# One transformer block on one core: unit 0's front made by the generator of the later units, the operand sums of the down weights dealt to other engines, unit 2's statistics and load at other places

## The chip, the core and the metric

The kernel runs on one core of a Trainium2 chip. TensorE (PE) multiplies matrices and transposes; VectorE (DVE), ScalarE (ACT) and GpSimd (POOL) do the element-wise work; the queue of SyncE (SP) issues the transfers. Each engine works through a queue of its own in order, and semaphores hold an instruction until what it needs is done. The metric is the device time of one execution in microseconds (us); lower is better.

## The reference, cut to what matters

All is fp32. `x` is (4, 2048, 512): T = 4 steps of 2048 columns with 512 features. The context has 77 rows of 512 for each of the 4 steps; there are 16 heads of 32.

```python
def _layernorm(x): return (x - mean(x)) / sqrt(var(x) + 1e-5)

def _L0_attn_ref(xs, ...):                    # recurrence over the 4 steps, 64 states
    u = einsum('hk,tbpk->tbph', Vinv * dt, x)
    z = einsum('hk,bpk->bph', V, A * z + u_t) # for each step t
    return 2.0 * ys.real

def _L0_xattn_ref(query, context, Wq, Wk, Wv, Wo):
    scores = einsum('bqhd,bkhd->bhqk', Q, K) / sqrt(32)
    return softmax(scores) @ V @ Wo.T         # heads joined

def _L0_ffn_ref(x, ...):
    h = butterfly(x @ W_exp + b_exp, up_weights)
    h = gelu(h + up_bias)
    h = butterfly(h, down_weights)
    return h @ W_con + b_con + down_bias

x = x + _L0_attn_ref(_layernorm(x), ...)
x = x + _L0_xattn_ref(_layernorm(x), ctx_1024, ...)
x = x + _L0_ffn_ref(_layernorm(x), ...)
```

The butterflies are linear, so they can be multiplied into `W_exp` and `W_con`.

## The kernel before, in words

**Units.** The 2048 columns are cut into 16 units of 128; a unit is one tile `xt` of 128 columns x 4 steps x 512 features. A unit has a *front* (recurrence, cross attention) and a *feed-forward*. The products of a front (queries `q`, output `w`) and the up product are done as seven block products in place of eight; the down product is done with 26 block products out of sums of blocks of either operand.

**Two stretches.** The *opening* (0 to 194.6 us) multiplies the butterflies into the weights (the generator `prep`, made by `_prepare`), makes keys and values, and does unit 0's front and the first part of unit 1's. Then `feed_forward(u)` runs for u = 0 to 15, and between its products it takes one `step()` of the generator `front(u + 1)`, so that PE has the next unit's attention between the products of this one.

**Order.** PE goes in the order of the program throughout. SP and POOL do so in the opening only. DVE and ACT always, and SP and POOL after the opening, are ordered by the framework's scheduler, with some instructions pinned by `keep_in_program_order`.

**Unit 0's front (`front_first`, L646).** It was written by hand, apart from `front`. `normed_pairs` makes the rows for the recurrence one pair ahead (tag `xn`, two buffers), L626 transposes them; `normed` does so for the query rows (L584, L593) and, on ACT, for the final rows (L582). `seven` does the seven query products (L641) with the adds of L676, and POOL changes `b21` (L683) after the second. In attention each of the 4 steps t has four score products (L704); DVE takes the minimum (L707), and ACT does 16 exponentials, each with its sum as a by-product (L709). `divided` takes the reciprocal and multiplies on DVE (L693, L695). Then come transposes of the probabilities (L723), copied to `pt` (L726, L728), and the values (L735). The output products are again `seven`, added to `xt` at L755.

**The other units' front (`front`, L788).** Rows are made two pairs ahead. In attention DVE takes the minimum (L904) and subtracts it (L905), ACT does one exponential over all 16 heads (L908), DVE sums and takes reciprocals (`weighed`, L890), and divides one half of the heads; POOL divides the other (L894). Query product 6 uses a bank of tag "a", the others tag "f". Two sets of transposes are made for one tile `pt`, and values are done two steps at a time. `normed_rows(wait, ...)` makes normalised rows and waits that many steps before it transposes them (L840). `next_stats` takes the next unit's statistics.

**`combine` (L993)** makes the sums of blocks of the normalised rows that the up products read: `t1`, `t2` on DVE, `t3` (L999) and `n4` (L1001) on POOL. For unit 0 it was called after the opening.

**Preparing the weights.** `prep` is stepped through by hand, in turns with `first` (unit 0's front). Its late steps are: the up weights' sums and stores (L474 to L478), 16 groups that multiply the high stages of the down butterfly (L488), 16 sets of transposes (L496, two to a step), and 16 final products (L502, blocks of `wdn`). `evict` copies a bank out; of `share[0]` evictions two are on DVE and the rest on ACT: `share[0]` is 5, and 6 behind the L488 loop.

**The operand sums.** The 26 block products of the down stage need sums of blocks of the down weights: for each j of 0 to 3 two lots of nine (`RIGHT`), made by `_right_sums` (L142 on POOL, L144 on DVE) in two `rings`, and stored by `_right_stores` (L154) to `dn26` in DRAM. Lots use the same two rings again and again, so a lot of j + 1 waits for the store of the same ring for j. j = 0 is made in the opening, and j = 1, 2, 3 in the first three rounds p of unit 0's `feed_forward`. j = 0 and 1 are all on POOL; for j = 2 and 3 the eight sums named in `FAST` are on DVE and ten on POOL.

**Unit 0's up products.** Round p has `up_head` (products 1, 6, 5), `up_mid` (2, 7) and `up_tail` (4, 3), the last one round late (L1028). Product 6 is followed by the add `u2` (L1047), product 7 by `u3` (L1059, L1060). Product 7 of p = 0 is the fifth in the order of PE; it adds into the bank that L1047 reads, and reads `t3`. The weights of rounds 0 and 1 are loaded in the opening (`w_first`, `w_second`), later ones by `up_weights`. Unit 1's query weights (L849) go to the buffer of `w_first`.

Of the kernel before, what the change touches and what calls it, by code (L numbers as in the profile page):

```python
# [17 lines left out]
P = 128  # L18
# [65 lines left out]
FAST = "24", "5", "1", "8", "14", "2", "20", "10"  # L84
# [48 lines left out]
def _right_sums(nc, j, wdn, rings, alone):  # L133

    made = {f"b{k}{d}": wdn[:, 4 * j + k, d * (D // 2) : (d + 1) * (D // 2)] for k in range(4) for d in range(2)}
    for lot, ring in zip(RIGHT, rings):
        w = ring.rearrange("p (s d) -> p s d", s=len(lot))
        for i, (name, x, op, y) in enumerate(lot):
            made[name] = w[:, i, :]
            x, y, op = made[x], made[y], ALU.add if op == "+" else ALU.subtract  # L140
            if alone or name not in FAST:
                nc.gpsimd.tensor_tensor(made[name], x, y, op)  # L142
            else:
                nc.vector.tensor_tensor(made[name], x, y, op)  # L144
# [215 lines left out]
def _prepare(nc, keep, pool, room, late, banks, dram, ident, wexp_t, up_low, up_high, up_bias, dn_low, dn_high, wcon,  # L360
# [122 lines left out]
    nc.sync.dma_start(out=brow[1, :].rearrange("(p m) -> p m", m=NB), in_=b2)  # L483
    for c in range(NC):
# [7 lines left out]
    share[0] = 6  # L492
# [22 lines left out]
def kernel(ctx: ExitStack, tc: tile.TileContext, x, ctx_t, ssm_vec, ssm_vt, ssm_vinv, wq_t, wk_t, wv_t,  # L515
# [54 lines left out]
    def normed(xt, res, steps, by_act):  # L570

        mv, y = norm_stats(xt)
        nb = shifts(mv, y) if by_act else None
        xnt = work.tile([P, NC, T, P], F32, tag="xnt", bufs=2, name="xnt")
        for _ in range(steps):
            yield
        rows = {}

        def row(t):
            rows[t] = work.tile([P, D], F32, tag="xn", name="xn")  # L580
            if by_act:
                nc.scalar.activation(rows[t], xt[:, t, :], AF.Identity, bias=nb[:, t : t + 1], scale=y[:, t : t + 1])  # L582
                return
            nc.vector.tensor_scalar(rows[t], xt[:, t, :], mv[:, t, 0:1], y[:, t : t + 1], ALU.subtract, ALU.mult)  # L584

        row(0)
        for t in range(T):
            if t + 1 < T:
                row(t + 1)
            yield  # L590
            ps = psum.tile([P, NC, P], F32, tag="f", name="ps_t")
            for c in range(NC):
                nc.tensor.transpose(ps[:, c, :], rows[t][:, c * P : (c + 1) * P], ident)  # L593
            nc.scalar.copy(xnt[:, :, t, :], ps)
        res.append(xnt)

    def normed_pairs(xt, res, stats, by_act):


        mv, y = stats  # L600
        nb = shifts(mv, y) if by_act else None
        xpt = work.tile([P, T // 2, D // NS, P], F32, tag="xnt", bufs=2, name="xpt")
        half = D // 2
        yield
        rows = {}

        def row(n):
            i, h = divmod(n, 2)
            rows[n] = work.tile([P, NC, 2, NS], F32, tag="xn", name="xp")
            for k in range(2):  # L610
                t = 2 * i + k
                out, x = rows[n][:, :, k, :], xt[:, t, h * half : (h + 1) * half].rearrange("p (f n) -> p f n", n=NS)
                if by_act:
                    nc.scalar.activation(out, x, AF.Identity, bias=nb[:, t : t + 1], scale=y[:, t : t + 1])
                else:
                    nc.vector.tensor_scalar(out, x, mv[:, t, 0:1], y[:, t : t + 1], ALU.subtract, ALU.mult)

        row(0)
        for n in range(T):
            i, h = divmod(n, 2)  # L620
            if n + 1 < T:
                row(n + 1)
            yield
            ps = psum.tile([P, NC, P], F32, tag="f", name="ps_t")
            for f in range(NC):
# [20 lines left out]
    def front_first(xt, res, wq):  # L646
# [51 lines left out]
        for t in range(T + 1):  # L698
# [30 lines left out]
            if t < T:  # L729
                divided(*probs[t])  # L730
# [620 lines left out]
```

## Time and profile before

| what | us |
|---|---|
| median of 3 runs | 2517.42 (2515.62 to 2520.43) |
| the profiled execution | 2515.81 |
| its span | 2514.0 |
| PE busy | 2473.6 |
| opening, up to the first up product (L1028) | 194.57 |
| first final product (L502) | 168.82 |
| unit 1's first query product (L870) | 221.99 |

The span is what the profiler recorded of the execution; 1.8 us lie around it. Busy times are per engine, and they overlap. A row of waits names the engine and line that waited, the instruction that ended the wait, and the us in total, how often, and the longest. A row of stretches gives busy time of each engine within the stretch. A row of the timeline gives the start, the time, the engine, the line, the operation, and in brackets how long the engine had been idle and what released it.

### The profile page before, as it was taken

What the parts mean: (1) busy time and instruction counts of PE and PEld (TensorE: products, weight loads), DVE (VectorE), ACT (ScalarE), POOL (GpSimd) and SP (SyncE); (2) the same over time, 40 slices, a digit from 0 to 9 for tenths busy, and PEclk for the clock granted to TensorE, in tenths of its full rate; (3) what the DMA queues carried; (4) which work ended last, traced back from release to release, by engine and by line L of the source; (5) the groups of instructions that cost most, each with busy time, mean ns of one, the idle gap of its engine ahead of it and who ended that gap; (6) DMA issues with size and microseconds to landing.
All of it is one profiled execution on the core that took longest, in us unless ns stands there. A gap on an engine that the chain in (4) does not pass through costs nothing.

```text
span 2514.0 us, 38070 instructions
## 1 busy us (share of the span) xinstructions
PE 2473.6 (98%) x14246; PEld 2138.3 (85%) x14246; DVE 1646.9 (66%) x3827; ACT 845.2 (34%) x1497; POOL 997.1 (40%) x945
## 2 busy tenths in 40 slices
PE   7899999999999999999999999999999999999999
PEld 5767888888888888888888888888888888888888
DVE  7666677576675757667576666757666675865643
ACT  2453424142342413334241333415133341423321
POOL 4535433515243251524325152342515144261534
PEclk9999999999999999999999999999999999999999
DMA  6727463635546364564626446463644636264457
GB/s 200 264 101 271 157 229 101 219 125 168 201 147 222 101 213 143 160 209 139 230 93 206 158 153 216 137 219 106 196 156 162 217 128 228 101 193 147 157 195 249
DMA packets 291860, 441.27 MB, mean 176 GB/s; under 512 B 20969, under 2 KB 248489, under 8 KB 287325
## 3 DMA queue, kind: packets, MB, share of 16 engines
q1 hardware_dynamic: 291678, 438.85, 52.2%
q8 instruction: 114, 1.87, 0.3%
q14 instruction: 68, 0.56, 0.1%
HBM read 398.30 MB, written 39.86 MB: 174 GB/s over the span
## 4 chain that ended last, share of the span: by engine, by line
PE 93%; DVE 3%; POOL 1%; DMA 1%; ACT 1%; issue 1%; SPq 0%; DVEq 0%; ACTq 0%; POOLq 0%
PE ps_b L1028 13%; PE ps_a L1126 13%; PE ps_c L1028 9%; PE ps_a L1028 8%; PE ps_b L1126 8%; PE ps_q L870 7%; PE ps_w L870 7%; PE ps_c L1126 7%; PE ps_sc L901 5%; PE ps_pt L917 4%; PE ps_s L808 3%; PE ps_o L931 2%; PE ps_t L840 2%; PE ps_t L799 1%; POOL arena L142 1%; PE ps_p L448 1%
## 5 line engine op out<-in xcount | busy, mean ns | idle before, releaser
L1081 POOL TENSOR_TENSOR arena<-arena 128x512 f32<-128x512 f32 x448 | 568.7, 1276 | 536.1 <-ACT arena L1033 273.9
L1033 ACT ACTIVATE arena<-arena,hbias 128x256 f32<-128x256 f32 x384 | 189.9, 506 | 386.7 <-DVE arena L1068 231.2
L1028 PE MATMUL ps_b<-arena 128*128 128x256 f32 x1128 | 289.8, 379 | 0.0
L1028 PEld LDWEIGHTS ps_b<-arena 128*128 128x128 f32 x1128 | 205.3, 190 | 28.5
L1126 PE MATMUL ps_a<-arena 128*128 128x256 f32 x896 | 214.2, 380 | 3.6 <-DVE xt L1141 3.6
L855 POOL TENSOR_TENSOR tq<-xnt 128x512 f32<-128x512 f32 x15 | 19.0, 1268 | 444.1 <-ACT xnt L841 444.1
L1028 PE MATMUL ps_a<-xnt,arena 128*128 128x256 f32 x752 | 193.1, 379 | 0.0
L894 POOL TENSOR_TENSOR pr<-pr,sm 128x616 f32<-128x616 f32 x60 | 100.3, 1671 | 226.0 <-DVE sm L893 188.4
L1126 PEld LDWEIGHTS ps_a<-arena 128*128 128x128 f32 x896 | 165.4, 190 | 24.6 <-DVE xt L1141 4.6
L1126 PE MATMUL ps_b<-arena 128*128 128x256 f32 x768 | 183.8, 379 | 0.0
L901 PE MATMUL ps_sc<-kbd,qt 128*128 128x308 f32 x480 | 163.7, 423 | 1.0 <-DVE pr L905 1.0
L1126 PEld LDWEIGHTS ps_b<-arena 128*128 128x128 f32 x768 | 144.7, 190 | 19.0
L1126 PE MATMUL ps_a<-w,arena 128*128 128x256 f32 x640 | 159.6, 381 | 0.0
L1028 PEld LDWEIGHTS ps_a<-xnt,arena 128*128 128x128 f32 x752 | 138.4, 190 | 20.2
L904 DVE TENSOR_REDUCE low<-ps_sc 128x4 f32<-128x308 f32 x240 | 114.4, 477 | 53.9 <-PE ps_sc L901 47.8
L917 PE MATMUL ps_pt<-ident,pr 128*77 128x128 f32 x960 | 144.0, 273 | 0.3 <-DVE pt L922 0.3
L917 PEld LDWEIGHTS ps_pt<-ident,pr 128*77 128x77 f32 x960 | 123.2, 148 | 23.1 <-POOL xt L1101 0.6
L870 PE MATMUL ps_q<-xnt,wq 128*128 128x256 f32 x600 | 141.7, 379 | 0.0
L827 ACT ACTIVATE xn<-xt,mv,y 128x512 f32<-128x512 f32 x44 | 34.6, 811 | 298.3 <-DVE mv L567 298.3
L1126 PEld LDWEIGHTS ps_a<-w,arena 128*128 128x128 f32 x640 | 117.9, 190 | 18.1 <-issue 2.8
L870 PEld LDWEIGHTS ps_q<-xnt,wq 128*128 128x128 f32 x600 | 114.0, 190 | 15.5
L974 DVE TENSOR_TENSOR xt<-ps_w,xt 128x512 f32<-128x512 f32 x90 | 60.4, 689 | 97.9 <-PE ps_w L870 97.9
(263 smaller groups left out, 5113.7 us busy)
## 6 DMA issues: line engine op xcount, KB each, us to landing
arena<-dn SPq DMA_DIRECT2D x256, 512.0 KB, 4.8
w<-dn SPq DMA_DIRECT2D x160, 512.0 KB, 4.4
arena<-up SPq DMA_DIRECT2D x79, 896.0 KB, 4.4
wq<-wq SPq DMA_DIRECT2D x16, 1792.0 KB, 9.7
w<-up SPq DMA_DIRECT2D x32, 896.0 KB, 7.3
xt<-in_x SPq DMA_DIRECT2D x11, 1024.0 KB, 6.7
dn<-arena SPq DMA_DIRECT2D x8, 1152.0 KB, 4.1
out<-xt SPq DMA_DIRECT2D x33, 256.0 KB, 2.5
```

The source lines that it names most:

```text
L808: nc.tensor.matmul(ps[:, 2 * i : T, f * NS : (f + 1) * NS], lhsT=xpt[:, i, c * (P // NS) + f, :], rhs=gt[:, 0 : T - 2 * i, :], start=i == ...
L840: nc.tensor.transpose(ps[:, c, :], rows[t][:, c * P : (c + 1) * P], ident)
L870: nc.tensor.matmul(tiles[key][:, r, :], lhsT=lhs(i, r, k), rhs=rhs(i, k), start=key == i and r == 0 and k == 0, stop=k == 1, skip_group_ch ...
L894: by.tensor_tensor(pr[:, h], pr[:, h], sm[:, h].unsqueeze(2).to_broadcast([P, NH // 2, NK]), ALU.mult)
L901: nc.tensor.matmul(ps[:, 0 : 4 * NK], lhsT=qt[:, g, t, :], rhs=kbd[:, t, g, :], start=True, stop=True)
L904: nc.vector.tensor_reduce(low, sc, AX.X, ALU.min)
L917: nc.tensor.transpose(ps[0:NK, j, :], probs[t][0][:, 4 * g + j, :], ident)
L974: nc.vector.tensor_tensor(r, ps, r, ALU.add)
L1028: nc.tensor.matmul(ps, lhsT=w[:, c, :], rhs=rhs[i - 1][:, c], start=first and c == 0, stop=c == 1, skip_group_check=True)
L1033: nc.scalar.activation(out, x, AF.Gelu, bias=hbias[:, b : b + 1])
L1081: nc.gpsimd.tensor_tensor(place(p), place(x), place(y), ALU.add if op == "+" else ALU.subtract)
L1126: nc.tensor.matmul(ps, lhsT=left[:, j, :], rhs=pair[:, n, j, :], start=first and j == 0, stop=j == NB // 4 - 1, skip_group_check=True)
```

## The change

1. `front_first`, `normed`, `normed_pairs` and `seven` are gone. Unit 0 goes through `front`, with the query weights handed in, one wait step before the query rows and six before the final ones. So its attention takes the form that the other units have. `combine` of unit 0 comes at the end of that generator, inside the opening.
2. Tiles of tag `xn` have four buffers in place of two.
3. `_right_sums` takes one engine for all 18 sums of a j: POOL for j = 0 and 1, DVE for j = 2 and 3. `FAST` is gone.
4. `share[0]` is 8 from before the L488 loop on.
5. In the opening's loop over the last steps of `prep` the turns are dealt anew: two steps of `first` per step of `prep` up to n = 26, then one of `first` and one of `second` (unit 1's front) up to n = 35, then `first`. Unit 1's statistics move from n = 17 to n = 22, the load of `w_first` from 17 to 22, that of `w_second` from 25 to 28, and the loads of `ybias` and `db` from 15 to 3.
6. Unit 2's `x` is loaded at p = 5 in place of 6, and its statistics are taken after the values of steps 0 and 1 in `front(1)`, in place of its end; its first rows are no longer made at the end of `front(0)`.

```diff
-def _right_sums(nc, j, wdn, rings, alone):
+def _right_sums(engine, j, wdn, rings):
...
-            if alone or name not in FAST:
-                nc.gpsimd.tensor_tensor(made[name], x, y, op)
-            else:
-                nc.vector.tensor_tensor(made[name], x, y, op)
+            engine.tensor_tensor(made[name], x, y, op)
...
+    share[0] = 8
     for c in range(NC):
         for g in range(4):
...
-    share[0] = 6
...
-    def front_first(xt, res, wq):
...
-            rows[n] = work.tile([P, NC, 2, NS], F32, tag="xn", name="xp")
+            rows[n] = work.tile([P, NC, 2, NS], F32, tag="xn", bufs=4, name="xp")
...
-    def front(u, xt, res):
+    def front(u, xt, res, wq=None):
 
         by_act = u == 1
+        if not u:
+            stats[0] = norm_stats(xt)
         pair, rows = pairs.pop(u) if u in pairs else first_rows(xt, stats.pop(u), by_act)
...
-        if by_act:
+        if u < 2:
             yield
...
-            if last and u == 1:
-                next_stats()
...
-        wq = work.tile([P, 7, NC // 2, D // 2], F32, tag="pt", bufs=1, name="wq")
-        tc.keep_in_program_order(nc.sync.dma_start(out=wq, in_=wq7))
-        xnt = yield from normed_rows(12 if u == 1 else 9, by_act, False)
+        if u:
+            wq = work.tile([P, 7, NC // 2, D // 2], F32, tag="pt", bufs=1, name="wq")
+            tc.keep_in_program_order(nc.sync.dma_start(out=wq, in_=wq7))
+        xnt = yield from normed_rows((1, 12, 9)[min(u, 2)], by_act, False)
...
-                         "a" if i == 6 else "f")
+                         "a" if u and i == 6 else "f")
...
                 values(0)
                 values(1)
+                if u == 1:
+                    next_stats()
...
-        xnt = yield from normed_rows(14 if u == 1 else 10, True, True)
+        xnt = yield from normed_rows((6, 14, 10)[min(u, 2)], True, True)
         res.append((u, xt, xnt))
         combine(xnt, res)
-        if u + 1 < NU:
+        if u and u + 1 < NU:
             pairs[u + 1] = first_rows(xts[u + 1], stats.pop(u + 1), False)
...
             if u == 0 and p < 3:
-                _right_sums(nc, p + 1, wdn, rings, p == 0)
+                _right_sums(nc.vector if p else nc.gpsimd, p + 1, wdn, rings)
                 _right_stores(nc, p + 1, wdn, rings, dn26, (0, 1, 2))
...
-            if p == (1 if u else 6) and u + 2 < NU:
+            if p == (1 if u else 5) and u + 2 < NU:
                 xts[u + 2] = load_x(u + 2)
...
-        for _ in range(6):
+        for _ in range(8):
             run(prep, first)
-        run(prep, prep, first, first, first, first)
+        next(first)
         for n, _ in enumerate(prep):
-            if n == 17:
-                stats[1] = norm_stats(xts[1], tc.keep_in_program_order, tc.keep_in_program_order)
-            if n == 27:
-                _right_sums(nc, 0, wdn, rings, True)
-            if n == 31:
-                _right_stores(nc, 0, wdn, rings, dn26, (2, 0))
-            if n not in (24, 25):
-                next(first, None)
-            if n > 31:
-                next(second)
+            run(*((first, first) if n < 27 else (first, second) if n < 36 else (first,)))
             if n == 3:
...
+                db = work.tile([P, D], F32, tag="xn", bufs=4, name="db")
+                nc.sync.dma_start(out=ybias, in_=b_con.partition_broadcast(P))
+                nc.sync.dma_start(out=db, in_=down_bias.partition_broadcast(P))
+                nc.gpsimd.tensor_tensor(ybias, ybias, db, ALU.add)
             if n == 15:
                 xts[1] = load_x(1)
                 second = front(1, xts[1], ready)
...
+            if n == 22:
+                stats[1] = norm_stats(xts[1], tc.keep_in_program_order, tc.keep_in_program_order, ahead="_next")
+                early.append(work.tile([P, 7, 2, P], F32, tag="pt", bufs=1, name="w_first"))
+                nc.sync.dma_start(out=early[0], in_=up7[0])
+            if n == 27:
+                _right_sums(nc.gpsimd, 0, wdn, rings)
+            if n == 28:
                 early.append(work.tile([P, 7, 2, P], F32, tag="qt", bufs=1, name="w_second"))
                 nc.sync.dma_start(out=early[1], in_=up7[1])
...
+            if n == 31:
+                _right_stores(nc, 0, wdn, rings, dn26, (2, 0))
-        for _ in first:
-            pass
...
-    combine(ready[0][2], ready)
```

## The prediction

> **What bounds the kernel now.** I read the page first, then TensorE's waits up to 260 us, then busy time by stretch, then the timeline around the place where unit 0 hands over from the opening to its feed-forward.
>
> ```profile
> span 2514.0 us, 38070 instructions
> PE 2473.6 (98%) x14246; PEld 2138.3 (85%) x14246; DVE 1646.9 (66%) x3827; ACT 845.2 (34%) x1497; POOL 997.1 (40%) x945
> PE 93%; DVE 3%; POOL 1%; DMA 1%; ACT 1%; issue 1%; SPq 0%; DVEq 0%; ACTq 0%; POOLq 0%
> ```
>
> PE is busy for all but 40.4 us, and the chain of waits is PE. The matmuls are the same ones in both kernels, in another order, so the only things to be won or lost are PE's waits and its clock. From 400 to 2200 us the stretches show PE busy 300.00 of each 300 us; what can change lies before 260 us.
>
> ```profile
> PE ps_k L277 <- DMA wk<-in_wk_t: 7.8, 1, 7.8
> PE ps_pt L723 <- DVE pt L728: 3.9, 7, 0.8
> PE ps_t L626 <- DVE xp L616: 2.9, 3, 1.2
> PE ps_b L1028 <- DVE arena L1047: 2.3, 1, 2.3
> PE ps_q L641 <- POOL xnt L683: 2.3, 1, 2.3
> PE ps_t L593 <- ACT xn L582: 1.6, 1, 1.6
> PE ps_t L840 <- ACT xn L827: 1.5, 1, 1.5
> PE ps_o L735 <- ACT pt L726: 1.3, 2, 0.9
> PE ps_b L1028 <- DVE arena L1059: 0.9, 1, 0.9
> ```
>
> Columns: who waited for whom, us in total, times, the longest. L277 waits for the first load, which the change leaves alone. L626, L641, L723 and L735 are unit 0's hand-written front; L1028 and L840 are the handover.
>
> ```profile
> 203.00:206.00 3.00, 2.39 (x10) 1.83 (x11) 2.13 (x6) 0.51 (x1) 1.96 (x3) 1.00 1.05 323
> 206.00:209.00 3.00, 0.71 (x4) 0.28 (x2) 1.96 (x4) 0.00 (x0) 1.97 (x3) 1.00 0.92 303
> 209.00:212.00 3.00, 2.98 (x8) 2.12 (x8) 3.00 (x7) 0.00 (x0) 3.00 (x4) 0.60 1.04 438
> 212.00:215.00 3.00, 1.50 (x6) 1.24 (x6) 1.78 (x7) 2.51 (x5) 0.11 (x1) 0.50 1.07 360
> 215.00:218.00 3.00, 3.00 (x10) 2.42 (x10) 1.28 (x3) 2.56 (x7) 2.04 (x3) 0.50 0.94 401
> 220.00:250.00 30.00, 30.00 (x140) 26.03 (x140) 17.92 (x33) 11.53 (x20) 8.40 (x10) 1.00 0.63 244
> ```
>
> Columns: the stretch, busy us of PE, PEld, DVE, ACT, POOL, then PE's granted clock, DMA share, GB/s. After the wait of 2.31 us the clock falls to 0.50 and is back at about 219.8: 10.3 us at half speed, which costs 5.2.
>
> ```profile
> 207.04 0.99 DVE L144 TENSOR_TENSOR arena<-arena 128x256 f32<-128x256 f32 x1 [1.91 <-issue]
> 208.55 0.41 DVE L1047 TENSOR_TENSOR arena<-ps_b,arena 128x256 f32<-128x256 f32 x1
> 189.40 15.71 POOL L142 TENSOR_TENSOR arena<-arena 128x256 f32<-128x256 f32 x21
> 210.63 0.42 SPq L849 DMA_DIRECT2D wq<-wq x1
> ```
>
> From the timelines: the add L1047, for which PE waits 2.3 us, stands in DVE's queue behind an operand sum (L144), which waits for the store that frees its ring. POOL makes one such sum in 0.748 us. The load of the next unit's query weights (L849) is issued at 210.63, and its first product runs at 221.99, 11.4 us later.
>
> **Anchors.** T0 is the first final product (L502, at 168.82). H is unit 1's first query product (L870, at 221.99); behind it PE is full, apart from 1.0 us near 253. I work out both anew.
>
> **Part 1, the opening up to T0.** *Removed.* The waits of unit 0's queries and attention: L723 3.9, L641 2.3 and 1.2, L735 1.6, the score products 0.8, L488 0.4: 10.2. A wait also costs a pipeline restart that counts as busy: from 89.37 to T0 PE is busy 69.1 us, while its work at undisturbed pitches is 14 products at 1.73 (q and w), 32 groups at 0.44 (pt and L496), 16 of L488 at 0.89, 16 scores at 0.52, 4 values at 1.0: 64.8. The other 4.3 goes with the waits. Of L626's 2.9 I take 2.0, since two pairs of rows stand ready and four buffers hold them (ends 0 and 2.9). *Moved.* Two w products, 3.5 us, slide behind T0; two query products slide ahead of 89 us, where PE is busy 28.17 of 29.37 anyway: nothing.
>
> *Added.* Unit 0 now has the steady softmax: 16 subtractions (0.48) and 8 sum-reduces (0.74) more on DVE, half of each divide on POOL (1.67, L894), one exponential of 1.23 for sixteen small ones at 0.30. Per t DVE has 4 x (0.47 + 0.48) + 2 x 0.74 + 0.4 + 0.75 = 6.4 us, before 3.6. PE runs 9 steps of the front and half as many groups of `prep` per t, some 8.9 us, so on average it fits. It doesn't at the first two t: there `prep` still makes the up weights' sums. Against one query product, 8 scores and 5 groups (1.73 + 4.2 + 4.5 = 10.3) DVE has 8 pairs (7.6), ten sums at 0.45 (4.5), an eviction and a query add (1.4) and the first softmax (2.6): 16.1. PE waits the 5.8 difference, for two score banks. Smaller waits of 0.2 to 1.5 for banks and evictions make 3.3 more when I step through both queues, and restarts 1.7: 10.8 (ends 5 and 15). The softmax of the later t and the fewer DVE evictions (2 of 8) cost nothing: PE's 8.9 us per t hides them; without that cover they'd be 2.8 us per t.
>
> T0: 168.8 - 10.2 - 4.3 - 2.0 - 3.5 + 10.8 = 159.6.
>
> **Part 2, T0 to the fifth up product (`up(0,7)`).** PE took 25.75 us to the feed-forward; now 3.5 (the two products) is added, waits of 1.63, 0.70, 0.27 go, and one for unit 0's final rows stays (statistics 4.0 us beside POOL's sums, then ACT 0.8; I take 1.9): 28.4, and 3.45 for four up products: T0 + 31.9.
>
> But `up(0,7)` needs two things. POOL's queue now holds all 36 sums ahead of L999's subtraction. They begin at T0 + 1.7, stop after three for a block that PE makes behind the moved products (T0 + 7.6), and take 33 x 0.745 = 24.6: T0 + 32.2; L999 ends at 33.5. Later still is DVE: the j = 2 sums (L144) wait for the store of the second ring, issued after POOL's last sum and 4.1 to 4.4 us long: T0 + 36.7. Behind the waiting sum stand two more sums, four tiny statistics and then L1047: T0 + 38.9. So PE waits 7.0 us where it waited 0.45. Behind that sum on SP wait the loads of the third up weights; they land before PE gets there.
>
> **Part 3, to H.** A 7 us wait is followed, as the 2.31 one was, by half clock: four products at 1.73 (to 45.8), two more (49.3), and the clock returns. The second frees the buffer of the query weights; DVE's seven sums and statistics there (4.3 us) hide under the slow products. Then 7.8 us of PE work stand before H, but the load takes 9.7 (median landing on the page) and some 0.8 around it: H = T0 + 59.8, against 53.2 before.
>
> The Trainium skill ("TensorE: Matmul & The Clock Gate", "HAM oscillation") warns of idle gaps over about 3.4 us; this trace throttled after 2.31, so the measurement goes ahead of it, and both halve the clock after 7 us. The same page has the clock back after about 3.4 us of activity, where the rows show 10.3. By the page H would be near T0 + 57, and the whole 2.8 us faster than my sum.
>
> H = 159.6 + 59.8 = 219.4, 2.6 earlier. The last edits (third unit's load at p = 5, its statistics after the values) touch no wait shown and cost nothing: PE is full there, and DVE has 12 of 30 us free from 220 to 250; without this cover they'd be 4 us of statistics. The profiled run is 2515.8 (span 2514.0 and 1.8 around it), 1.6 under the median of 2517.4: **2514.8 us** on the median's scale, 0.1% faster.
>
> **The rivals.**
> *The handover heals (faster).* If DVE's sums don't hold L1047, PE waits only for POOL (33.5, a wait of 1.6), and the opening's new waits are the 5 of the lower end. For: PE needs just one add. Against: the sum stands ahead of it in the built queue. T0 = 153.8; with the load of the weights still limiting, H = T0 + 54 = 207.8 at best; half of this way gives 2509, which I take as its time.
> *DVE's queue holds the handover longer (slower).* The place is the j = 2 sum that waits for the ring's store. The tile dn's DMAs land in
>
> ```profile
> DMA to landing us min/median/max: 3.6/4.7/15.7
> ```
>
> and the loads of the up weights now share that moment. At the longest it is 11.6 us later than my 4.1; from 2.6 us later on the gain is gone. Price: 2514.8 + 11.6 - 2.6 = about 2524. Against: the earlier stores land in 4.1 to 4.4.
> *The opening is bound by DVE (waits only change places).* The new waits reach the upper end 15: T0 164, and 2514.8 + 4.2 = 2519. For: DVE is 16.1 against 10.3 at the worst place. Against: ACT is freed of 16 exponentials.
>
> **How the numbers follow.** About 0.2%, 5 us, is what can be told from no change here. My forecast has 0.42 (2510 to 2520: 0.12 of it over the bound of faster, 0.30 same), the healed handover 0.26 (all faster), the held queue 0.20 (slower by over 5: all), the DVE-bound opening 0.12 (0.04 same, 0.08 slower). Sums: faster 0.38, same 0.34, slower 0.28. The range runs from 2505, a little beyond the healed time, to 2525, the held queue's: the forecast's own is 2510 to 2520.
>
> **What would show it.** L723's and L641's waits gone, new ones of score products (L701 of the changed kernel) on DVE adding to 5 to 6 us near 100 to 112; T0 near 160; POOL's 36 sums in one row of some 25 us; one wait of about 7 us at the fifth up product on L849's add; a clock of 0.50 behind it; H near 219. Wrong if T0 is above 165, if that wait is under 3 us or over 12, or if PE waits behind H by more than 2 us.

## The result, and the profile after

| | median, us | runs | beside before |
|---|---|---|---|
| before | 2517.89 | 15 (2515.62 to 2521.33) | |
| after | 2523.66 | 15 (2522.99 to 2526.02) | 1.0022 (95%: 1.0014 to 1.0030) |

The changed kernel is 5.8 us slower, 0.22%. The prediction had said 2514.8, that is 0.1% faster. Line numbers from here on are those of the kernel named, and each shifts a little with its edits.

First the page of the kernel after: span, busy times, and the shares of the chain of waits.

```profile
span 2521.6 us, 37902 instructions
PE 2476.3 (98%) x14246; PEld 2138.5 (85%) x14246; DVE 1664.1 (66%) x3867; ACT 832.8 (33%) x1377; POOL 985.5 (39%) x929
PE 93%; DVE 5%; ACT 1%; DMA 1%; issue 1%; POOL 0%; SPq 0%; DVEq 0%
```

PE has the same 14246 matmuls, and outside its busy time there are 45.3 us in place of 40.4. The profiled run of before lay 2 us under its median, so the two profiles differ by 7.6 us where the medians differ by 5.8. DVE's share of the chain rose from 3 to 5%.

PE's waits of the kernel after, over the whole span (who waited for whom, us in total, times, longest):

```profile
PE ps_t L600 <- ACT xp L579: 11.7, 1, 11.7
PE ps_k L273 <- DMA wk<-in_wk_t: 8.7, 1, 8.7
PE ps_sc L701 <- DVE pr L705: 5.6, 5, 3.7
PE ps_a L928 <- DVE xt L943: 2.6, 11, 0.6
PE ps_b L830 <- DVE w L556: 2.1, 1, 2.1
```

The waits of the old front (L723 and L641 of before) are gone. L701, the score products, is the wait that the prediction expected. The other rows are not as it had them: one of 11.7 us before unit 1's first transposes (L600) where 1.9 was set, eleven small ones of the down products (L928) where none was expected, and 2.1 at the fifth up product (L830) where 7.0 was expected. For the last the profile names L556, which DVE started only 0.23 us before PE went on; the add that the product needs, L849, runs right ahead of it (209.73).

The same places in the two profiled executions, in us (each is the start of a product on PE's timeline):

| place | before | after | difference | forecast |
|---|---|---|---|---|
| T0, first final product | 168.82 | 163.00 | -5.8 | -9.2 |
| first up product | 194.57 | 204.59 | +10.0 | -6.6 |
| H, unit 1's first query product | 221.99 | 225.77 | +3.8 | -2.6 |
| unit 2's first query product | 380.0 | 382.3 | +2.3 | -2.6 |
| unit 15's first query product | 2297.8 | 2305.3 | +7.5 | -2.6 |

So there are three parts: H is 3.8 late; 1.5 comes back on the way to unit 2; and then each of 13 units takes 147.92 us in place of 147.52, 5.2 in all.

**The 11.7 us.** ACT's timeline of the kernel after, around that wait (start, us, engine, line, operation, and in brackets the idle time before and its releaser):

```profile
181.09 1.52 ACT L628 ACTIVATE xn<-xt,mv,y 128x512 f32<-128x512 f32 x2 [8.53 <-DVE mv L563]
182.51 2.06 ACT L579 ACTIVATE xp<-xt,mv,y 128x256 f32<-128x256 f32 x4
```

L579 makes unit 1's rows, for which PE waits. Their statistics had been ready since 172.7. In ACT's queue they stand behind two of unit 0's final rows (L628), and these wait for unit 0's last statistics. ACT stands still for 8.5 us with work behind the head of its queue. Why those statistics were late, DVE's timeline of the kernel after shows:

```profile
170.06 0.68 DVE L776 TENSOR_TENSOR xt<-ps_w,xt 128x512 f32<-128x512 f32 x1
...
178.36 0.65 DVE L556 TENSOR_TENSOR w<-y,v 128x4 f32<-128x4 f32 x1
...
180.40 0.65 DVE L563 SCALAR_TENSOR_TENSOR mv<-mv,y 128x4 f32<-128x4 f32 x1
```

The last add of unit 0's output ends at 170.7. The fourteen operations on 4 columns behind it run from 172.71 to 181.05, most of them 0.65 each, while POOL makes its operand sums.

**The 0.40 us per unit.** DVE's timeline of before in a steady unit:

```profile
488.72 0.43 DVE L1141 TENSOR_TENSOR xt<-ps_a,xt 128x256 f32<-128x256 f32 x1 [1.32 <-PE ps_a L1126]
489.23 2.77 DVE L782 TENSOR_SCALAR xp<-xt,mv,y 128x256 f32<-128x256 f32 x4
491.92 1.75 DVE L998 TENSOR_TENSOR arena<-xnt 128x512 f32<-128x512 f32 x1
493.60 0.41 DVE L1141 TENSOR_TENSOR xt<-ps_a,xt 128x256 f32<-128x256 f32 x1
```

The same place in the kernel after:

```profile
489.59 3.95 DVE L581 TENSOR_SCALAR xp<-xt,mv,y 128x256 f32<-128x256 f32 x4
493.46 0.41 DVE L943 TENSOR_TENSOR xt<-ps_a,xt 128x256 f32<-128x256 f32 x1
493.79 2.41 DVE L581 TENSOR_SCALAR xp<-xt,mv,y 128x256 f32<-128x256 f32 x4
496.12 0.68 DVE L800 TENSOR_TENSOR arena<-xnt 128x512 f32<-128x512 f32 x1
496.72 0.41 DVE L943 TENSOR_TENSOR xt<-ps_a,xt 128x256 f32<-128x256 f32 x1
```

The next unit's rows (L782, now L581) are four halves before and eight after: with four buffers the scheduler places the later pairs sooner, ahead of the adds of the down products (L1141, now L943) that free PE's banks. PE's timeline of the kernel after, in the same place, shows one of the waits:

```profile
497.19 1.99 PE L928 MATMUL ps_a<-arena 128*128 128x256 f32 x8 [0.18 <-DVE xt L943]
```

In the kernel before these eight products and the eight ahead of them follow without a break:

```profile
492.85 3.62 PE L1126 MATMUL ps_a<-arena 128*128 128x256 f32 x16
```

From 400 to 1000 us PE is now busy 599.33 of 600, where it was busy all the time before: the gaps are 0.16 us per unit. The rest of the 0.40 counts as busy PE at the same place. Before, the sixteen products take 3.46 us up to the next one (at 496.31); after, 3.90 (from 495.12 to 499.02). The weight loads of the same products wait for DVE too: 7.4 us in thirteen waits from 400 to 2400 us (5.2 in nine and 2.2 in four), none before.

### The profile page after: what moved, and what is told of

Same layout as the page of the kernel before. It is cut to its first block, busy times and chain, and to the rows that moved or that the text cites. A ratio compares the mean times of both kernels' runs of the same rounds, so it can differ in the third digit from the quotient of the medians.

```text
span 2521.6 us, 37902 instructions
## 1 busy us (share of the span) xinstructions
PE 2476.3 (98%) x14246; PEld 2138.5 (85%) x14246; DVE 1664.1 (66%) x3867; ACT 832.8 (33%) x1377; POOL 985.5 (39%) x929
## 4 chain that ended last, share of the span: by engine, by line
PE 93%; DVE 5%; ACT 1%; DMA 1%; issue 1%; POOL 0%; SPq 0%; DVEq 0%
PE ps_b L830 13%; PE ps_a L928 12%; PE ps_c L830 9%; PE ps_a L830 9%; PE ps_b L928 8%; PE ps_w L670 8%; PE ps_q L670 8%; PE ps_c L928 7%; PE ps_sc L701 5%; PE ps_pt L717 4%; PE ps_s L609 3%; PE ps_o L731 2%; PE ps_t L639 2%; DVE xp L581 1%; PE ps_t L600 1%; PE ps_p L444 1%
## 5 line engine op out<-in xcount | busy, mean ns | idle before, releaser
L830 PE MATMUL ps_b<-arena 128*128 128x256 f32 x1128 | 289.8, 379 | 0.0
L830 PEld LDWEIGHTS ps_b<-arena 128*128 128x128 f32 x1128 | 205.3, 190 | 28.5
L928 PE MATMUL ps_a<-arena 128*128 128x256 f32 x896 | 217.7, 381 | 3.2 <-DVE xt L943 2.6
L694 POOL TENSOR_TENSOR pr<-pr,sm 128x616 f32<-128x616 f32 x64 | 106.7, 1667 | 245.4 <-DVE sm L693 184.7
L830 PE MATMUL ps_a<-xnt,arena 128*128 128x256 f32 x752 | 193.1, 379 | 0.0
L928 PEld LDWEIGHTS ps_a<-arena 128*128 128x128 f32 x896 | 164.3, 190 | 28.7 <-DVE xt L943 7.2
L928 PE MATMUL ps_b<-arena 128*128 128x256 f32 x768 | 183.7, 379 | 0.0
L701 PE MATMUL ps_sc<-kbd,qt 128*128 128x308 f32 x512 | 175.2, 425 | 6.6 <-DVE pr L705 5.6
L928 PEld LDWEIGHTS ps_b<-arena 128*128 128x128 f32 x768 | 144.7, 190 | 19.0
L928 PE MATMUL ps_a<-w,arena 128*128 128x256 f32 x640 | 159.6, 381 | 0.0
L704 DVE TENSOR_REDUCE low<-ps_sc 128x4 f32<-128x308 f32 x256 | 121.8, 477 | 56.8 <-PE ps_sc L701 50.7
L830 PEld LDWEIGHTS ps_a<-xnt,arena 128*128 128x128 f32 x752 | 138.4, 190 | 20.2
L717 PE MATMUL ps_pt<-ident,pr 128*77 128x128 f32 x1024 | 153.0, 273 | 1.3 <-ACT pt L720 0.7
L670 PE MATMUL ps_q<-xnt,wq 128*128 128x256 f32 x640 | 151.4, 379 | 0.9 <-DMA wq<-wq 0.6
L717 PEld LDWEIGHTS ps_pt<-ident,pr 128*77 128x77 f32 x1024 | 130.8, 148 | 24.9 <-ACT pt L720 0.9
L628 ACT ACTIVATE xn<-xt,mv,y 128x512 f32<-128x512 f32 x48 | 35.5, 804 | 306.8 <-DVE mv L563 306.8
L670 PEld LDWEIGHTS ps_q<-xnt,wq 128*128 128x128 f32 x640 | 121.2, 190 | 18.0 <-ACT arena L835 0.9
L776 DVE TENSOR_TENSOR xt<-ps_w,xt 128x512 f32<-128x512 f32 x99 | 66.4, 689 | 101.8 <-PE ps_w L670 101.7
L928 PEld LDWEIGHTS ps_a<-w,arena 128*128 128x128 f32 x640 | 117.9, 190 | 18.1 <-issue 2.8
```

Of the source, the lines that this page charges most:

```text
L670: nc.tensor.matmul(tiles[key][:, r, :], lhsT=lhs(i, r, k), rhs=rhs(i, k), start=key == i and r == 0 and k == 0, stop=k == 1, skip_group_ch ...
L694: by.tensor_tensor(pr[:, h], pr[:, h], sm[:, h].unsqueeze(2).to_broadcast([P, NH // 2, NK]), ALU.mult)
L701: nc.tensor.matmul(ps[:, 0 : 4 * NK], lhsT=qt[:, g, t, :], rhs=kbd[:, t, g, :], start=True, stop=True)
L704: nc.vector.tensor_reduce(low, sc, AX.X, ALU.min)
L717: nc.tensor.transpose(ps[0:NK, j, :], probs[t][0][:, 4 * g + j, :], ident)
L776: nc.vector.tensor_tensor(r, ps, r, ALU.add)
```

## The experiments

Each was run beside the kernel before on the same chip; the table has medians in us and the ratio to that before, with its 95% interval.

| kernel | this | before | ratio |
|---|---|---|---|
| e1: after, later rows pinned | 2516.26 | 2518.37 | 0.9993 (0.9984 to 1.0001) |
| e2: before, four buffers | 2522.46 | 2518.37 | 1.0015 (1.0006 to 1.0024) |
| e3: after, unit 1's rows first on ACT | 2525.87 | 2518.37 | 1.0030 (1.0019 to 1.0042) |
| e4: after, POOL's sums later | 2521.63 | 2518.37 | 1.0012 (1.0003 to 1.0021) |
| e5: e1 + e3 + unit 0's rows three steps later | 2510.19 | 2518.28 | 0.9969 (0.9957 to 0.9980) |
| e6: e5, other sums pinned | 2516.25 | 2518.28 | 0.9992 (0.9983 to 1.0001) |
| e7: e5, sums dealt as before | 2514.01 | 2518.28 | 0.9983 (0.9974 to 0.9992) |
| e8: before, sums dealt as after | 2516.04 | 2518.28 | 0.9990 (0.9981 to 0.9999) |
| e9: e5, all pairs of unit 1 first | 2505.49 | 2517.95 | 0.9947 (0.9934 to 0.9961) |
| e10: e9, sums dealt in turn | 2512.87 | 2517.95 | 0.9976 (0.9967 to 0.9986) |
| e11: e9, part 6 undone | 2510.68 | 2518.56 | 0.9963 (0.9950 to 0.9977) |
| e12: e9, evictions shared as before | 2511.03 | 2518.56 | 0.9968 (0.9955 to 0.9980) |

### Four buffers: e1 and e2

e1 keeps the later two pairs of rows of units 2 and up where the program has them on DVE; `PAIRS[2:]` are those pairs, and `later` is set behind the opening:

```diff
-                    nc.vector.tensor_scalar(o, x, mv[:, t, 0:1], y[:, t : t + 1], ALU.subtract, ALU.mult)
+                    made = nc.vector.tensor_scalar(o, x, mv[:, t, 0:1], y[:, t : t + 1], ALU.subtract, ALU.mult)
+                    if later[0] and n in PAIRS[2:]:
+                        tc.keep_in_program_order(made)
```

> The changed kernel, but the third and fourth pair of rows of each unit from 2 on may not be made ahead of the down product's last adds (they keep their place in the program on DVE); the four buffers stay. Theory (four buffers let DVE make eight row halves instead of four ahead of the add that frees PE's bank, 0.40 us per unit): the pitch of the units returns from 147.92 to 147.52 us, the DVE waits of the down products at the last bank go, and the time falls by 5 to 6 us, to 2518. Rival (the whole loss sits in the opening, the steady pitch is noise or clock): 2523.7, within 1.

e2 gives the kernel before only the four buffers, at each of the tiles of tag `xn`:

```diff
-            rows[n] = work.tile([P, NC, 2, NS], F32, tag="xn", name="xp")
+            rows[n] = work.tile([P, NC, 2, NS], F32, tag="xn", bufs=4, name="xp")
```

> The kernel before with nothing changed but four buffers for the tag xn. Theory (buffers alone slow the steady units): pitch 147.9 us, time 2517.9 + 5 = 2523. Rival (the pitch comes from another part of the change, such as the statistics' place): 2517.9, within 1.

e1 takes 147.49 us per unit, as before; its span is 5.5 us shorter than that of after, and its median some 7. The 11.7 us wait stays in it. e2 takes 147.9 per unit and is 4.1 us slower than before by the medians. PE's waits of e2, the row of the down products:

```profile
PE ps_a L1126 <- DVE xt L1141: 5.8, 9, 4.5
```

The 4.5 is one wait in unit 0's down stage, which is 3.2 in the kernel before; the other eight are the small ones, and before has none of them from 400 to 2400 us. The loss of the steady units was given by the buffers alone and taken by pinning the rows that they set free. This is shown from both sides.

### The 11.7 us: e3, e4 and e5

e3 starts unit 1's front at n = 22, so that its first rows come ahead of unit 0's final rows in ACT's queue:

```diff
-            run(*((first, first) if n < 27 else (first, second) if n < 36 else (first,)))
+            run(*((first, first) if n < 27 else (first, second) if 27 < n < 36 else (first,) if n == 27 else (first,)))
...
                 stats[1] = norm_stats(xts[1], tc.keep_in_program_order, tc.keep_in_program_order, ahead="_next")
+                next(second)
```

> The changed kernel with unit 1's first rows handed to ACT ahead of unit 0's final rows (front(1) is started at n = 22), so they no longer stand behind rows that wait for unit 0's statistics. Theory (the statistics themselves are late, the queue of ACT only decides where PE notices): the wait of 11.7 us at L600 shrinks to 2 or 3, but one of 8 to 9 appears 2.6 us of work later, at the transposes of unit 0's final rows; time 2521 to 2523. Rival (ACT's order is the cause): the wait goes, 10 us less at the handover, 2514 to 2516.

PE's waits of e3:

```profile
PE ps_t L639 <- ACT xpt L601: 6.4, 1, 6.4
PE ps_q L670 <- DMA wq<-wq: 4.9, 1, 4.9
...
PE ps_t L600 <- ACT xp L579: 2.0, 1, 2.0
```

The wait for unit 1's rows falls from 11.7 to 2.0, and 6.4 comes up at the transposes of unit 0's final rows (L639), which stand next in PE's order. Those rows are made from 181.91 on, behind the same statistics, and the copy L601 that frees the bank for L639 stands behind them on ACT (183.34). So ACT's order alone was not the cause: PE's own order had it wait for the late rows next. A load of the query weights, issued at 214.32 right behind one of up weights at 213.90, adds 4.9 us, and e3 ends 2 us slower than after, above the times of its theory and of its rival.

e4 makes POOL's first lot of sums, and its stores, at n = 33 in place of 27 and 31:

```diff
-            if n == 27:
+            if n == 33:
                 _right_sums(nc.gpsimd, 0, wdn, rings)
...
-            if n == 31:
+            if n == 33:
                 _right_stores(nc, 0, wdn, rings, dn26, (2, 0))
```

> The changed kernel with the sums of j = 0 issued at n = 33 in place of 27 (their first stores with them), so that POOL makes none while DVE takes unit 0's final statistics. Theory (POOL's sums hold up DVE's small operations): the fourteen small operations take some 3 us in place of 8.3, the wait at L600 shrinks from 11.7 to about 6, but all 36 sums start some 15 us later and hold the handover instead: 2524 to 2532. Rival (the statistics are late for the length of their own chain): the operations stay at 0.65 us each and the wait at 11.

DVE's timeline of e4, two of the operations that took 0.65 each in the kernel after:

```profile
175.81 0.17 DVE L557 TENSOR_TENSOR w<-w,y 128x4 f32<-128x4 f32 x1
...
176.21 0.16 DVE L563 SCALAR_TENSOR_TENSOR mv<-mv,y 128x4 f32<-128x4 f32 x1
```

PE's waits of e4:

```profile
PE ps_t L600 <- ACT xp L579: 5.0, 1, 5.0
PE ps_b L830 <- DVE arena L849: 3.9, 1, 3.9
```

With POOL silent the fourteen operations take 2.6 us in place of 8.3, and the wait falls by 6.7. So of the 11.7 us 6.7 come from POOL's sums running beside the small operations. 3.9 of it are given back at the handover: POOL's sums now run from 195.2 to 214.5, beside the next small statistics on DVE, which take up to 0.70 each there, and the add L849 stands behind these (206.73). The time is 2 us under after, and under the 2524 to 2532 of the theory.

e5 joins e1 and e3 and gives unit 0's final rows nine wait steps:

```diff
-        xnt = yield from normed_rows((6, 14, 10)[min(u, 2)], True, True)
+        xnt = yield from normed_rows((9, 14, 10)[min(u, 2)], True, True)
```

> e1's kernel with unit 1's first rows ahead on ACT (as in e3) and unit 0's final rows transposed three steps later (nine waits in place of six), so that unit 1's transposes and recurrence products fill the time in which unit 0's statistics are made. Theory (unit 0's late statistics cost the opening some 10 us, and with that gone the wait forecast for the handover appears): no wait over 3 us between the first final product and the feed-forward, the feed-forward starts 10 us sooner than the 206 of e1, near 195, and the fifth up product then waits 5 to 8 us for the add behind the operand sums; time 2509 to 2512. Rival (the handover is bound by something earlier, so the whole 10 us come out): 2505. Rival (nothing gained, the wait moves to the handover in full): 2516.

e5 is 6 us faster than e1. Of the wait 7.7 is left (5.7 at the third pair of unit 1, again behind unit 0's final rows on ACT). Its first up product starts at 201.52 and the fifth at 205.22 without a wait: the wait of 5 to 8 us at the handover did not appear. H is 218.73.

### The deal of the sums: e6, e7, e8 and e10

e6 pins all sums of j = 1 to 3 in the program's order, so that none stands ahead of an add that PE waits for:

```diff
-            engine.tensor_tensor(made[name], x, y, op)
+            keep(engine.tensor_tensor(made[name], x, y, op))
...
-                _right_sums(nc.vector if p else nc.gpsimd, p + 1, wdn, rings)
+                _right_sums(nc.vector if p else nc.gpsimd, p + 1, wdn, rings, tc.keep_in_program_order)
```

> e5's kernel with the operand sums of j = 1, 2, 3 kept in their place of the program on their engine: POOL makes t3 and n4 ahead of the 18 sums of j = 1, and DVE's sums stand behind the adds of their round. Theory (the sums ahead of t3 and of the add make the handover's wait): the fifth up product waits under 2 us, and 4 to 6 us come off e5, 2505 to 2508, unless the late stores then hold the weights of the up products or the ring's reuse. Rival (DVE stands in the queue behind ring stores anyway): no difference from e5.

It is 6 us slower than e5; neither the theory nor the rival held. POOL's timeline of e6:

```profile
199.33 1.78 POOL L803 TENSOR_TENSOR arena<-xnt 128x512 f32<-128x512 f32 x1 [17.48 <-ACT xnt L642]
```

POOL waits 17.5 us for the rows that `t3` reads, with 18 sums behind it that could have run. Those run from 202.96 to 215.9 then, beside unit 1's small statistics on DVE. The add for the fifth up product (L851) stands behind statistics that take up to 0.69 each, and PE waits 2.1.

e7 is e5 with the old deal (j = 2, 3: eight sums on DVE, ten on POOL), and e8 is before with the new one:

```diff
+FAST = "24", "5", "1", "8", "14", "2", "20", "10"
...
-            engine.tensor_tensor(made[name], x, y, op)
+            (engine if name in FAST else pool_).tensor_tensor(made[name], x, y, op)
```

> e5's kernel with the operand sums dealt as in the kernel before (for j = 2 and 3 eight on DVE, ten on POOL). If the new deal is worth something by itself, this is slower than e5; theory (where the sums of j = 1 stand decides, not who makes those of j = 2 and 3): the same as e5 within 2 us. Rival (the new deal is what costs the handover): 3 to 6 us faster than e5.

```diff
-            if alone or name not in FAST:
+            if alone or j < 2:
                 nc.gpsimd.tensor_tensor(made[name], x, y, op)
```

> The kernel before with the new deal of the operand sums alone. Theory: the waits of the handover of the kernel before (5.5 us and 10 us of half clock) came from sums on DVE that wait for a ring; with 18 in place of 8 there they stay, within 2 us of 2518. Rival (the new deal frees POOL and heals the handover): 2512 to 2514. Other rival (it alone makes the loss): 2522 to 2525.

The new deal is worth 3.8 us in e5: with the old one PE waits 2.8 for the add of the fifth up product. In the kernel before it is worth 2.2: the handover's waits of 2.3 and 0.9 go, and one of 3.6 comes up for a load of up weights. So part 3 of the change is a gain in both, though in e8 the interval only just leaves out 1. Both theories fell in what they said: e7 is not the same as e5, and in e8, whose time is at the edge of the theory's, the waits did not stay.

e10 deals the lots in turn (j = 0 and 2 on POOL, 1 and 3 on DVE), over e9, which follows below:

```diff
-                _right_sums(nc.vector if p else nc.gpsimd, p + 1, wdn, rings)
+                _right_sums(nc.gpsimd if p == 1 else nc.vector, p + 1, wdn, rings)
```

> e9's kernel with the operand sums dealt by turns: j = 0 and 2 on POOL, j = 1 and 3 on DVE, so that j = 1 is made on DVE while POOL still makes j = 0 or just after. Theory (the limit at the handover is POOL's 36 sums in a row and the store behind them): the second ring of j = 1 is stored by 195, u2 is done when the fifth product needs it, the wait there stays under 1.5 us, the feed-forward's first query product comes at 211 to 214, and the time is 2502 to 2506. Rival (DVE's sums beside POOL's are held up by the same port and stand in the way of unit 1's adds): 2509 to 2515.

It is 7 us slower than e9, in the range of its rival. PE's timeline of e10 at the fifth up product:

```profile
205.06 2.04 PE L837 MATMUL ps_b<-arena,w_first 128*128 128x256 f32 x4 [3.65 <-DVE arena L856]
206.90 1.91 PE L837 MATMUL ps_a<-xnt,w_second 128*128 128x256 f32 x4
```

Here POOL's lot of j = 2 falls on unit 1's small statistics on DVE: they take up to 1.18 each between 200.5 and 204.4, and the add L856 behind them comes at 204.49. Four matmuls then take 1.9 to 2.0 in place of 1.03: half the clock.

### The version that beats both: e9

e9 is e5 with unit 0's final rows pinned on ACT behind all four pairs of unit 1's rows:

```diff
+                    one = nc.scalar.activation(rows[t], xt[:, t, :], AF.Identity, bias=nb[:, t : t + 1], scale=y[:, t : t + 1])
+                    if not u:
+                        tc.keep_in_program_order(one)
...
+            early_wait = wait - 3 if last and not u else 0
+            for _ in range(early_wait):
+                yield
             row(0)
             row(1)
-            for _ in range(wait):
+            for _ in range(wait - early_wait):
                 yield
```

> e5's kernel with unit 0's final rows handed to ACT only behind all four pairs of unit 1's rows, pinned there, so that the wait of 5.7 us of e5 at unit 1's third pair goes as well. Theory (the handover has a limit of its own: u2 at 204.7 in e5, behind 36 sums on POOL, the store of a ring and sums on DVE; PE came to it at 205 only because the opening was late): no wait over 2.5 us in the opening, the feed-forward starts at 194 to 196, the fifth up product waits 4 to 7 us for L851's add at 203 to 205, the clock halves once, time 2509 to 2512, the same as e5 within 1.5. Rival (the add comes sooner when PE comes sooner): 2503 to 2505.

It is the fastest: 12.5 us under before and 18 under after. PE's waits of e9:

```profile
PE ps_sc L708 <- DVE pr L712: 5.7, 5, 3.7
PE ps_s L611 <- ACT xpt L603: 2.9, 1, 2.9
PE ps_t L602 <- ACT xp L579: 2.4, 2, 2.0
```

POOL's timeline of e9, and behind it PE's at the fifth up product:

```profile
171.31 23.20 POOL L140 TENSOR_TENSOR arena<-arena 128x256 f32<-128x256 f32 x33 [1.85 <-ACT arena L378]
```

```profile
201.23 1.10 PE L837 MATMUL ps_b<-arena,w_first 128*128 128x256 f32 x4
```

POOL makes 33 sums without a pause, from T0 + 8.8 to T0 + 32.0 (T0 is 162.5 here). The first up product is at 197.54 and the fifth at 201.23, with less than 0.3 of a wait. H is 214.85, unit 2 begins at 369.8. My theory that the handover would hold it at the time of e5 fell: the add comes sooner when PE comes sooner, since what stands ahead of it moves too.

### Two parts once more, over e9: e11 and e12

e11 undoes part 6:

```diff
+            if last and u == 1:
+                next_stats()
...
-                if u == 1:
-                    next_stats()
...
-            if p == (1 if u else 5) and u + 2 < NU:
+            if p == (1 if u else 6) and u + 2 < NU:
```

> e9's kernel with unit 2's load and statistics put back where the kernel before has them (p = 6, and the end of front(1)). Theory (the wait of 3.2 us of the kernel before at one of unit 0's down products, on an add that stands behind work for unit 2 on DVE, is what this part of the change removes): the wait comes back near 340, unit 2's first query product is 2 to 3 us later, and the time is 2508 to 2509. Rival (what the prediction said: this part touches no wait): 2505.5 within 1.

It costs 5.2 by the medians, about 4 by the ratios. PE's timeline of e11, in unit 0's down stage:

```profile
339.10 6.70 PE L935 MATMUL ps_a<-arena 128*128 128x256 f32 x16 [3.85 <-DVE xt L950]
```

Sixteen matmuls take 6.70 in place of the 3.6 that they take elsewhere: half the clock behind the wait. In the kernel before there is such a wait (3.22 and 0.38), and part 6 shortens it (0.65 and 0.39 after). PE's other waits between H and unit 2 are 0.7 longer after, so 1.9 us less are waited there in all; that is about the 1.5 us that came back. e11 lost more, since the clock stayed full behind the wait in the kernel before, and halved in e11.

e12 puts the share of evictions on DVE back to two of five and two of six, where the change has two of eight (`share[0]` = 8):

```diff
-    share[0] = 8
     for c in range(NC):
...
+    share[0] = 6
     for n, b in enumerate(ORDER):
```

> e9's kernel with the evictions shared as in the kernel before (two of five on DVE in the loop of the down butterfly's products, two of six behind it, in place of two of eight). Theory (DVE is full only at the first two steps of unit 0's attention, where one or two evictions fall): 0 to 1.5 us slower, 2505 to 2507. Rival (the opening hangs on DVE throughout): 3 to 6 us slower.

It costs 5.5 by the medians, 5 by the ratios. PE's waits of e12:

```profile
PE ps_s L611 <- ACT xpt L603: 5.2, 1, 5.2
PE ps_q L677 <- DVE qt L691: 3.9, 2, 2.3
```

The first row was 2.9 in e9, but unit 1's first transposes wait 1.8 less in e12. The second holds one wait of 2.3 at 231.5, behind H, with the clock at 0.50 behind it. H is 216.0, where e9 has 214.9, and unit 2 begins at 375.2 in place of 369.8: most of the loss lies behind the opening. My theory of at most 1.5 fell; the size is that of its rival, but the place is not. DVE's timeline of e12 at that wait, and then that of e9 at the same place:

```profile
223.41 7.37 DVE L140 TENSOR_TENSOR arena<-arena 128x256 f32<-128x256 f32 x18 [1.03 <-DMA dn<-arena]
```

```profile
222.06 4.19 DVE L140 TENSOR_TENSOR arena<-arena 128x256 f32<-128x256 f32 x9 [0.87 <-DMA dn<-arena]
```

In e12 18 operand sums stand in a row ahead of the add L691 for which PE waits, in e9 nine. So the share of evictions acted there through the order on DVE; why the order came out so was not followed further.

## Why the prediction was wrong, by its steps

**Part 1, the front.** The waits removed and added were right: L723 and L641 gone, the new ones 9.6 us from 89 us to T0 where 9.1 was set, the largest on the score products because DVE is slower than PE at the first two t. Mis-sized were the restarts, 1.7 in the sum: from 90.69 to T0 PE is busy 62.6 us, 4.7 beyond the 57.9 that its work there comes to at the prices of the sum. The stretches of the kernel after, behind its three longer waits (PE, PEld, DVE, ACT, POOL, clock, DMA share, GB/s), show a part of why:

```profile
115.60:118.50 2.90, 2.86 (x10) 2.54 (x11) 1.23 (x3) 0.44 (x1) 0.00 (x0) 0.50 1.03 281
118.50:121.00 2.50, 2.50 (x21) 2.33 (x20) 1.66 (x3) 1.60 (x3) 0.00 (x0) 0.92 1.05 288
183.60:186.00 2.40, 2.36 (x6) 1.48 (x7) 0.00 (x0) 2.18 (x5) 0.00 (x0) 0.50 1.11 411
186.00:188.50 2.50, 2.50 (x12) 1.72 (x11) 0.00 (x0) 2.11 (x5) 1.20 (x2) 0.77 0.92 298
212.30:214.30 2.00, 2.00 (x6) 1.64 (x5) 1.93 (x9) 0.82 (x3) 0.00 (x0) 0.50 1.02 431
214.30:216.30 2.00, 2.00 (x10) 1.70 (x10) 0.42 (x1) 2.00 (x4) 0.00 (x0) 0.96 0.43 180
```

The 3.7 us wait for a score (it ends at 115.6) halves the clock for some 3.3 us, which costs 1.6. The prediction charged the half clock to the handover only. The other 1.4 of the 3.0 beyond the sum is not explained. T0 came 3.4 late of the forecast.

**Part 2, the step "one for unit 0's final rows stays (statistics 4.0 us beside POOL's sums, then ACT 0.8; I take 1.9)".** This is the step that failed in the opening: 11.7. (The terms of that sum also add up to 28.6, not 28.4; that is too little to matter.) The statistics took 8.3 us in their small operations alone (e4: 2.6 without POOL), and unit 1's rows stood behind unit 0's on ACT, which I had not listed. The half clock behind this wait, 3.5 us long, was not in the sum either. e3 shows that the order on ACT alone does not heal it, e5 and e9 that order and a later place together do.

**Part 2, the fifth up product.** POOL's sums and the late add were well placed in themselves: the end of the sums was set at T0 + 32.2 and is T0 + 32.0 in e9, the add at T0 + 38.9 and it runs at T0 + 38.2. For the add that is luck, at least in part: the prediction had DVE wait for a store there, and in e9 DVE stands ahead of the add without a pause from 194.59 on, in unit 1's statistics and other work. The wait of 7.0 did not come about in the kernel after, since PE got there 13.3 us later behind T0 than set (45.2 in place of 31.9), nor in e9, where smaller waits ahead (2.0, 0.4 and 2.9) and the longer way bring PE there at T0 + 38.7. What POOL's queue costs is paid a few us earlier, in DVE's small operations.

**Part 3.** The clock was right in kind: half behind each of these three waits. T0 to H took 62.8 us, set at 59.8: more from the 11.7, less from the 7.0 that stayed at 2.1 and the half clock that lasted 3.4 us behind it, where some 10 were set. H was 6.4 later than forecast, 3.4 from T0 and 3.0 from here.

**"PE is full there".** Two edits were costed at nothing behind H by this sentence, and both changed the time there. This is the step that failed behind the opening. Four buffers were used only for their gain in the opening; in the steady units they cost 0.40 us each, 5.2 in 13 (e1 and e2), which is two thirds of the difference of the profiles. A PE without a wait says nothing of how much the engine that frees its banks can be delayed: in the rows of before DVE did four row halves between two adds L1141 (488.72 and 493.60) and PE did not wait, after it eight stand about the same adds and PE waits. And part 6 was said to touch no wait shown; its wait of 3.2 us lay at 344.6, in unit 0's down stage, behind the 260 us at which I stopped reading PE's waits. That error was in the change's favour (1.5 here; 4 to 5 in e11, half clock included).

**The rivals.** None was what happened. The held queue came closest in time (2524), but its mechanism, the j = 2 sum that waits for the store, decided nothing; the DVE-bound opening came near at T0 (163.0, where it had 164 and the forecast 159.6), but that is only a part of the loss. Without the loss of the steady units (e1) the change would have come out at 0.9993 (0.9984 to 1.0001), inside the forecast's own range and not told from before; with the order of the rows mended as well (e5, e9) it is faster.

## What to carry to other kernels

More buffers are an edit to every loop that shares the tag: compare the order on each engine in a steady unit too, and ask which add or copy that frees a PSUM bank now stands behind the work set free. Where two streams share an in-order engine, look at what each head of the queue waits for; a row whose inputs are late belongs behind all the rows whose inputs are there, and moving the waiting work in PE's order as well is what makes it pay (e3 against e9). Read the waits of the whole span before a moved step is priced at nothing.

## What the runs showed of the hardware that was not expected

**Small operations beside GpSimd.** Operations on 128x4 values take 0.16 us alone and 0.65 beside POOL's sums (0.75 each), up to 1.18 in e10. Of the big ones, those that read one tensor or a PSUM bank hardly show it. The operand sums on DVE, with two inputs in SBUF, do: from 199.80 on five of them take 4.74 us in the kernel after, beside POOL, where one takes 0.42 alone. The Trainium skill ("SBUF — State Buffer", "Who interferes with whom") says that a VectorE instruction with two SBUF inputs contends with a GpSimd instruction that reads SBUF, and that the port pair that they share is locked for one of them at a time. The rows of the two-input operations (L556, L557, and the operand sums) agree: 0.65 is a little under one sum. But L551 to L553, which read one tensor, took 0.63 to 0.65 as well, though L554 took 0.15; in e4 it is L552 and L554 that take 0.70, and L551 and L553 0.17. That sentence does not cover them.

**The clock.** It halved behind waits of 2.09 (after), 2.29 (e12), 2.31 (before), 3.65 (e10), 3.68 (after), 3.85 (e11) and 11.7 us (after), but not behind one of 3.22 in the kernel before, on PE's timeline there, where eight matmuls take 1.99:

```profile
344.60 1.99 PE L1126 MATMUL ps_a<-arena 128*128 128x256 f32 x8 [3.22 <-DVE xt L1141]
```

Nor did it behind one of 2.28 there (it ends at 101.94), and a wait of 1.97 before unit 1's first transposes was followed by half clock in e5 and not in e9. So the length of the wait alone does not tell. Where it falls does: within each trace, the moments at which the granted clock changes lie whole multiples of 3.41 us apart. With the 14 traces divided into pieces of 3.41 us on this grid, from 20 us on, there are 42 falls to half clock. Of these 39 come behind a piece in which PE was idle for 1.97 us or more, the other three behind 1.32, 1.48 and 1.76; no piece with more than 1.95 left the clock full. The wait of 3.22 fell on two pieces, with 1.36 and 1.86 us idle. The clock came back behind every piece with at most 0.56 us idle, and behind none with 0.62 or more.

This also settles how long it stays down. The half clock lasted one piece behind the waits of 3.68 and 2.09 in the kernel after, two (6.8 us) in e10 and e11, where PE was still idle for 1.25 and 0.77 us of the first, and three in the kernel before, the 10.3 us from which the prediction took its price: there PE had more idle parts, 0.77 and 0.73 us in the first two pieces. The page that the prediction set aside ("TensorE: Matmul & The Clock Gate", "What's actually happening") has the clock back after about 3.4 us of activity, which is what these pieces show.
